# A graph transformer and a graph attention layer on one core: a new order for every step, and more buffers for five kinds of tiles

## Chip, cores and metric

The kernel runs on one core of a Trainium2 chip. The core has TensorE (PE), VectorE (DVE), ScalarE (ACT), GpSimd (POOL) and SyncE (SP), which here only issues DMAs. Each engine runs its own instructions strictly in the order in which the program lists them; engines wait for each other by semaphores. The metric is the device time of one execution in microseconds (us).

## What is computed

Two layers over 64 independent graphs of 256 nodes with 256 features. Layer 0 is a transformer layer whose attention is split by the value of the adjacency matrix; layer 1 is two graph attentions (GAT) and an FFN. Cut to what matters:

```python
# layer 0, per graph: x [256, 256], adj [256, 256]
q, k = heads(x @ Wq + bq), heads(x @ Wk + bk)                # 8 heads of 32
attn = softmax(q @ k.T / sqrt(32))
out  = sum(((attn * (adj == r)) @ heads(x @ Wv[r] + bv[r])) for r in range(4))
x1   = ln(x + merge(out) @ Wo + bo) * g1 + beta1
x2   = ln(x1 + gelu(x1 @ W1 + b1) @ W2 + b2) * g2 + beta2
# layer 1
def gat(h, W, a):
    Wh = h @ W
    e  = leaky_relu(Wh @ a[:256] + (Wh @ a[256:]).T, 0.2)
    return softmax(where(adj > 0, e, -9e15), axis=0) @ Wh
h  = ln(x2 + gat(gat(x2, gW1, ga1), gW2, ga2)) * g_ln1 + b_ln1
y  = ln(h + relu(h @ w_ff1 + b_ff1) @ w_ff2 + b_ff2) * g_ln2 + b_ln2
```

The adjacency holds only 0 and 1, so the kernel's main program handles those two values (a second program, for other values, stands behind a test and is not entered here).

## The kernel before

Weights stay in SBUF. There is no loop: the work of one graph is cut into some 210 named steps, and every step of every graph has a place, a number. `PLACES` gives the places for graph 0; graph g's step stands at `PLACES[name] + g * PERIOD`, with `PERIOD` 46.802. The program sorts all steps of all 64 graphs by place and emits them in that order. The places do nothing else: they are sort keys, and they set in which order each engine meets the steps of the six or seven graphs that are under way at once. The 49 weight loads (`LOAD_PLACES`) and the six pieces of weight preparation (`V_PLACE` and so on) are sorted into the same list. The numbers come from a search that was made beforehand.

The steps that the text names, in the order of the data, with the lines of the profile:

- `load`, `xT`, `cast`, `jT`, `no`: a graph's x and adjacency come in (L188, L190), are transposed (VectorE L527, a DMA transpose L543) and cast; `no` (GpSimd L550) is the mask of absent links for the GAT. `xS` (GpSimd L534): differences of blocks of x.
- `qk0`, `qk1`, `s0`, `s1` (TensorE L556, L604): queries and keys, and the scores of four heads each. `max`, `rec` (VectorE L609, L622), `exp`, `nrm` (ScalarE L617, L627): the softmax; the digits are the half m and the head h.
- `eT`, `eW`, `eR`: the attention is transposed in squares by VectorE (L338), written to DRAM and read back transposed (SyncE L343, L347). `pm` (VectorE L636) multiplies it by the adjacency: the mask. `po0`, `po1` (TensorE L651) and `oT0`, `oT1` (ScalarE L657): times the values.
- `vp1` to `vp7` (TensorE L580), `va` (VectorE L589), `vc1`, `vb`: the values, with seven products where eight blocks would be multiplied, and additions that put them together.
- `wo`, `ya` (TensorE L671, VectorE L675), `yb`: output projection and residual. Each layer norm n is `st` (VectorE L379), `rt`, `nb` (GpSimd L385 to L391), `ln` (ScalarE L396); `lg`, `lb` (GpSimd L363, L366) multiply and add its row vectors; `ag`, `ar`, `bg`, `br` are the same two operations on the residual of the FFN.
- FFN a (GELU): `aT`, `aW`, `aR` transpose as above; `at1` to `at4` (GpSimd L438) block differences; `ap1` to `ap7` (TensorE L453) seven products; `ac` (ScalarE L464) and `aa` (VectorE L470) put them together; `ax0` to `ax3` (ScalarE L476) the GELU; `aS1` to `aS4` (GpSimd L490) block differences of the hidden layer; `ad1` to `ad7` (TensorE L501) seven products; `ae`... (VectorE L509) add them to the residual. `tg` and `te` load ScalarE's tables.
- The GAT: `ga0`, `ga1`, `gac` (L681, L687), and for each of the two attentions A and B: `ip` (TensorE L693), `z` (ScalarE L700), `zl`, `zm`, `zx` (VectorE L703, L706, L710), `ze` (ScalarE L715), `zd` (L721, L723). `h1` and `h2` (TensorE L728, L743) are the products, `h1c`, `h2a` what reads them.
- FFN b (ReLU): `bu0` to `bu3` (TensorE L420), `bx0` to `bx3` (ScalarE L428), then `bS`, `bd`, `be` as in FFN a. `store` writes the result.

All products but the scores and a part of `ad` and `bd` share one kind of PSUM tile with three buffers (`ps_mm`); a step that opens one waits until the last reader of the buffer that it is given is done. The tiles that the change touches rotate in the same way in SBUF:

```python
plan += [(g * PERIOD + t, i, ops[n]) for i, (n, t) in enumerate(PLACES.items())]
with tc.manual_schedule():
    for _, _, f in sorted(plan, key=lambda p: p[:2]):
        f()
```

Of the kernel before, what the change touches and what calls it, by code (L numbers as in the profile page):

```python
# [9 lines left out]
F32 = mybir.dt.float32  # L10
# [8 lines left out]
P = 128  # L19
# [7 lines left out]

PERIOD = 46.802000
PLACES = {
    "load": 103.9751, "xT": 115.0053, "qk0": 126.6603, "qkc0": 127.1038, "s0": 134.9388, "max00": 136.7231,  # L30
    "qk1": 137.0310, "max03": 137.5321, "qkc1": 137.7942, "exp00": 138.1614, "max01": 140.5304, "rec00": 140.7033,
    "max02": 142.1718, "nrm00": 142.4292, "cast": 144.4484, "exp03": 147.8949, "eT00": 149.0132, "chk": 149.0607,
    "exp02": 149.5106, "exp01": 150.1354, "xS": 150.5393, "s1": 150.6950, "rec03": 150.7772, "nrm03": 151.8725,
    "max10": 153.8083, "max12": 153.8091, "max13": 154.4469, "eT03": 154.4477, "exp12": 154.6493, "eW03": 155.4630,
    "eW00": 156.5314, "rec01": 157.0565, "rec12": 158.9274, "rec02": 159.6382, "vp1": 161.4545, "nrm12": 165.5429,
    "max11": 166.0992, "vc1": 167.1785, "eT12": 168.1509, "nrm01": 168.3344, "jT": 169.8588, "eT01": 170.3657,
    "eW01": 171.0782, "exp10": 171.5535, "rec10": 172.2610, "exp13": 172.3736, "nrm10": 173.2351, "exp11": 174.3895,
    "eW12": 174.4820, "rec13": 177.1193, "eR03": 177.3099, "vp7": 177.3903, "vp6": 177.5917, "va6": 179.2791,
    "eR00": 179.4350, "va7": 180.4486, "nrm02": 180.6279, "eT10": 180.6555, "vb1": 180.6893, "nrm13": 180.6957,
    "vp5": 180.9267, "vp3": 181.2501, "va9": 181.6949, "eR01": 181.8420, "va5": 181.9831, "vp2": 182.0258,  # L40
    "va3": 182.1206, "va1": 182.7320, "eT02": 183.2926, "pm03": 183.3875, "vp4": 184.2094, "vb0": 187.0388,
    "va4": 187.0561, "eW02": 187.4248, "rec11": 187.7988, "eW10": 191.5046, "nrm11": 191.8443, "pm00": 193.2315,
    "eT13": 193.2323, "eR02": 195.3406, "eR10": 195.3413, "eT11": 196.6110, "pm01": 196.7514, "eW11": 197.3458,
    "y": 197.5444, "eW13": 204.3129, "pm02": 204.6352, "yb": 205.0770, "po0": 208.2558, "eR12": 211.7882,
    "pm10": 212.6028, "oT0": 213.3684, "pm12": 214.4221, "eR11": 215.4498, "eR13": 216.1883, "pm11": 220.8456,
    "pm13": 220.8464, "po1": 223.4844, "oT1": 225.7544, "wo": 226.4470, "ya": 228.2381, "st1": 228.8886,
    "rt1": 229.4475, "nb1": 229.9449, "ln1": 234.2672, "aT": 235.2647, "aW": 236.2517, "aR": 238.9482, "ag": 240.6661,
    "no": 243.1288, "at1": 243.2863, "at2": 243.3266, "ap1": 243.3672, "ap2": 243.9675, "ac1": 244.5699,
    "aa1": 245.3645, "ap6": 245.5386, "at3": 245.5532, "ac6": 247.4691, "at4": 247.9916, "ap7": 249.4691,
    "ar": 250.1780, "ap5": 250.3386, "ac7": 251.1468, "ap4": 251.5565, "aa7": 252.0569, "tg": 252.3489,  # L50
    "ap3": 252.4143, "ac4": 252.8450, "ax2": 253.7964, "aa6": 254.2113, "ax1": 256.9508, "ax0": 257.6471,
    "ax3": 257.7639, "aS1": 258.7003, "ad3": 259.1637, "ad5": 259.9822, "aS3": 260.0841, "aS2": 262.1691,
    "aS4": 262.4552, "ad1": 263.5703, "ad2": 263.5711, "ad7": 263.9317, "ad4": 265.6786, "ae": 265.7449,
    "ae1": 265.8658, "ae7": 266.1487, "ad6": 268.6987, "ae5": 269.4279, "ae6": 270.1012, "st2": 270.8366,
    "rt2": 272.8796, "nb2": 273.1259, "ln2": 275.0005, "lg2": 275.7094, "lb2": 276.1999, "hT": 276.2183,
    "hW": 280.2443, "hR": 282.2631, "ga0": 286.1421, "gac0": 286.2674, "ga1": 287.3134, "gac1": 287.4355,
    "ipA": 288.1844, "zA": 289.1647, "zlA": 290.9172, "zmA": 291.1840, "zxA": 291.3282, "zeA": 291.6948,
    "zdA": 291.8669, "h11": 293.6066, "h1c1": 294.2718, "h10": 295.3741, "h1c0": 297.1199, "ipB": 300.5575,
    "zB": 301.7395, "zlB": 303.5479, "zmB": 305.6801, "zxB": 305.9925, "zeB": 307.1002, "zdB": 307.5894,
    "h2": 312.8984, "h2a": 314.0704, "st3": 314.3871, "rt3": 315.0224, "nb3": 315.1133, "ln3": 316.3769,  # L60
    "bT": 317.8919, "bW": 321.5395, "bR": 322.2639, "bu1": 325.2576, "bu2": 326.9960, "bu0": 327.5659,
    "bx1": 327.8946, "bx2": 329.2876, "bu3": 329.6912, "bx0": 331.5281, "bg": 331.6469, "bx3": 332.3820,
    "br": 332.4081, "bS1": 332.4186, "bS2": 333.5718, "bd2": 334.8469, "bd3": 335.4834, "bd1": 335.5398,
    "bd6": 337.5839, "bS4": 340.4945, "bd5": 341.7280, "bS3": 342.6638, "be1": 344.6857, "be5": 345.2702,
    "be6": 345.5198, "bd4": 345.5393, "be": 346.8470, "bd7": 348.0359, "be7": 352.7953, "st4": 354.0792,
    "rt4": 357.7556, "nb4": 358.8382, "ln4": 359.6426, "lg4": 360.6282, "lb4": 364.9129, "store": 373.7957,
    "te": 514.9914,
}
LOAD_PLACES = [
    125.120, 106.258, 229.103, 150.870, 221.650, 221.641, 121.253, 228.780, 150.186, 119.871, 234.573, 232.294,  # L70
    235.866, 110.479, 215.936, 228.515, 130.114, 111.029, 155.377, 140.012, 185.331, 143.483, 182.314, 212.997,
    230.654, 163.446, 107.882, 259.336, 191.755, 270.022, 292.790, 266.477, 296.907, 276.387, 282.416, 241.872,
    305.973, 195.716, 294.339, 290.783, 243.026, 150.865, 294.400, 260.745, 293.271, 285.343, 296.910, 299.560,
    242.862,
]
V_PLACE, OUT_PLACE, FFA_PLACE, GAT_PLACE, FFB_PLACE, ODD_PLACE = 133.293, 191.755, 242.862, 282.414, 309.485, 240.000

# [11 lines left out]
def binary_graphs(  # L91
# [14 lines left out]
    B, N, D = x.shape  # L106
# [6 lines left out]
    C = N // P  # L113
# [6 lines left out]
    ap = ctx.enter_context(tc.tile_pool(name="attn", bufs=2))  # L120
    bp = ctx.enter_context(tc.tile_pool(name="dense", bufs=2))
# [29 lines left out]
    def weight(w, name, mixed=False):  # L151

        k, n = w.shape[0] // P, w.shape[1]
        t = const.tile([P, k, n], F32, name=name)
        if mixed:
            mixed_rows(t, w)
        else:
            loads.append((t, w.rearrange("(k p) n -> p k n", p=P)))
        return t
# [56 lines left out]
    wo, bo_r = weight(Wo, "wo"), rowvec(bo, D, "bo_r")  # L216
# [181 lines left out]
    class Ffn:  # L398
# [8 lines left out]
            self.t = self.xt = None  # L407

        def residual(self, src):
            self.r = bp.tile([P, C, D], F32, tag="res", name=f"{self.name}_res", bufs=3)  # L410
            times(self.r, src, self.gain)

        def residual_row(self):
# [17 lines left out]
        def node_sum(self, i):  # L431

            if self.xt is None:
                self.xt = bp.tile([P, 4, P], F32, tag="us", name=f"{self.name}_xt", bufs=1)
            (b11, b12), (b21, b22) = ([self.x.nodes(k)[:, j] for j in range(C)] for k in range(KD))
            t = [self.xt[:, j].rearrange("p (b y) -> p b y", y=S) for j in range(4)]
            o, a, b = {1: (t[0], b12, b11), 2: (t[1], b22, t[0]), 3: (t[2], b22, b12), 4: (t[3], b21, t[1])}[i]
            nc.gpsimd.tensor_tensor(o, a, b, ALU.subtract)  # L438
# [72 lines left out]
    class Graph:  # L511
# [99 lines left out]

        def exponential(self, m, h):
            n = f"{self.g}_{m}_{h}"
            self.e[m, h] = e = ap.tile([P, C, N], F32, tag="e", name=f"e{n}", bufs=4)
            self.den[m, h] = small.tile([P, C], F32, tag="den", name=f"den{n}")
            for ic in range(C):
                nc.scalar.activation(e[:, ic, :], self.s4[m][h][:, ic * N:(ic + 1) * N], AF.Exp,  # L617
                                     bias=self.nmax[m, h][:, ic:ic + 1], accum_out=self.den[m, h][:, ic:ic + 1])
# [8 lines left out]
                nc.scalar.activation(e[:, ic, :], e[:, ic, :], AF.Copy, scale=self.rden[m, h][:, ic:ic + 1])  # L627

        def squares(self, m, h):
            self.et[m, h] = Transposed(f"eT{self.g}_{m}_{h}", ap, "eT", 6)  # L630
            self.et[m, h].squares(self.e[m, h])

        def masked(self, m, h):
            t = self.et[m, h].t
            self.pm[m, h] = ap.tile([P, C, C, P], F32, tag="pm", name=f"pm{self.g}_{m}_{h}", bufs=4)
            nc.vector.tensor_tensor(self.pm[m, h].rearrange("p c k (b y) -> p (c k) b y", b=A),  # L636
                                    t.rearrange("p b c k y -> p (c k) b y"),
                                    self.adT.rearrange("p c k (b y) -> p (c k) b y", b=A), ALU.mult)
# [480 lines left out]
```

## Time and profile before

| | us |
|---|---|
| median of 3 runs | 3193.67 (3193.63 to 3193.97) |
| the profiled execution, and its span | 3193.6, 3191.7 |
| TensorE busy in the span | 3050.3 |
| span 0 to 167.4: TensorE busy | 129.0 of 167.4 |
| span 167.4 to 2981.5: TensorE busy | 2761.4 of 2814.1 |
| span 2981.5 to 3191.7: TensorE busy | 159.9 of 210.2 |

The three windows are the filling of the pipeline, the part in which every graph repeats the same pattern, and the draining. In the middle, windows of equal length one period apart show the same rows at the same distance, so one period stands for all. A row of a timeline gives the start, the length, the engine, the line, the tiles and the number of instructions that were merged; in brackets is the time that the engine idled before it and what ended the wait. The length of a matmul row is modelled, so the distance between starts is the better measure there.

### The profile page before, as it was taken

How to read it: one execution, taken by the hardware profiler on the slowest of the kernel's cores; microseconds unless marked ns; L12 is line 12 of the kernel's file. 1: busy time of each engine (PE TensorE's matmuls, PEld its weight loads, DVE VectorE, ACT ScalarE, POOL GpSimd, SP SyncE). 2: the span in 40 equal slices, each digit the busy share in tenths (PEclk: the TensorE clock that was granted, in tenths of full speed). 3: DMA queues.
4: the chain of work that ended last, by engine and by line, in shares of the span. 5: the costliest groups of instructions: out<-in, count | busy, mean ns of one | idle time of the engine just before them, and what ended most of it. 6: DMA issues, size and time to landing. Idle time of an engine off the chain costs nothing. (4 is left out here: it accounts for less than half of the span.)

```text
span 3191.7 us, 67685 instructions
## 1 busy us (share of the span) xinstructions
PE 3050.3 (96%) x23261; PEld 2626.8 (82%) x23261; DVE 2521.3 (79%) x5349; ACT 2479.2 (78%) x6853; POOL 2336.9 (73%) x2886
## 2 busy tenths in 40 slices
PE   6899999999999999999999999999999999999985
PEld 4788888888888888888888888888888888888774
DVE  6788888888878888888888888888888888888852
ACT  5678878878878877878887887887787787787752
POOL 2477777777777777777777777777777777777763
PEclk7999999999999999999999999999999999999997
DMA  6554455455455455455455455455455455455421
GB/s 190 156 151 141 145 154 145 140 154 147 142 151 147 141 152 150 139 153 152 136 155 151 138 152 152 138 149 153 137 150 154 138 147 154 142 143 154 136 63 31
DMA packets 808349, 456.88 MB, mean 143 GB/s; under 512 B 334528, under 2 KB 717376, under 8 KB 808000
## 3 DMA queue, kind: packets, MB, share of 16 engines
q1 hardware_dynamic: 808000, 452.49, 48.8%
q8 instruction: 187, 3.06, 0.4%
q14 instruction: 162, 1.33, 0.1%
HBM read 242.63 MB, written 201.33 MB: 139 GB/s over the span
## 5 line engine op out<-in xcount | busy, mean ns | idle before, releaser
L617 ACT ACTIVATE e<-s,nmax 128x256 f32<-128x256 f32 x1024 | 474.5, 480 | 73.0 <-DVE nmax L609 70.6
L420 PE MATMUL ffb_ps<-ffb_T,f 128*128 128x256 f32 x2048 | 459.2, 383 | 26.3 <-DMA ffb_T<-ffb_T_d 26.3
L627 ACT ACTIVATE e<-e,rden 128x256 f32<-128x256 f32 x1024 | 455.7, 503 | 11.6 <-DVE rden L622 11.6
L420 PEld LDWEIGHTS ffb_ps<-ffb_T,f 128*128 128x128 f32 x2048 | 389.9, 192 | 86.3 <-issue 17.2
L636 DVE TENSOR_TENSOR pm<-eT,adT 128x512 f32<-128x512 f32 x512 | 429.3, 849 | 4.3 <-DMA eT<-eT_d 3.7
L338 DVE STREAM_TRANSPOSE eT_sq<-e 128x512 f32<-128x512 f32 x512 | 359.7, 703 | 60.1 <-ACT e L627 35.8
L609 DVE TENSOR_REDUCE nmax<-s 128x2 f32<-128x512 f32 x512 | 331.4, 678 | 7.1 <-PE s L604 4.3
L565 ACT ACTIVATE qT<-qk_ps,bqs_c 128x256 f32<-128x256 f32 x128 | 60.7, 474 | 306.5 <-PE qk_ps L556 306.4
L490 POOL TENSOR_TENSOR ffa_t<-ffa_h 128x512 f32<-128x512 f32 x64 | 81.8, 1279 | 292.4 <-DVE gb_z L706 258.8
L428 ACT ACTIVATE ffb_h<-ffb_ps,bf_c 128x256 f32<-128x256 f32 x512 | 209.6, 483 | 28.4 <-PE ffb_ps L420 27.9
L476 ACT ACTIVATE ffa_h<-ffa_h,b_c 128x256 f32<-128x256 f32 x512 | 217.7, 501 | 2.2
L617 ACT ACTIVATION_READ_ACCUMULATOR e<-s,nmax 128x1 f32 x1024 | 216.7, 212 | 0.0
L386 POOL TENSOR_TENSOR rs_x<-rs_x,nhalf 128x2 f32<-128x2 f32 x256 | 200.7, 784 | 21.3
L490 POOL TENSOR_TENSOR ffa_t<-ffa_h,ffa_t 128x512 f32<-128x512 f32 x128 | 195.1, 1524 | 5.0
L490 POOL TENSOR_TENSOR ffb_t<-ffb_h 128x512 f32<-128x512 f32 x64 | 82.0, 1281 | 156.5 <-ACT ffb_h L428 156.5
L589 DVE TENSOR_TENSOR v<-v,v_ps 128x256 f32<-128x256 f32 x448 | 174.4, 401 | 10.1 <-PE v_ps L580 7.9
L396 ACT ACTIVATE ffa_res<-ffa_res,nb_x,rs_x 128x256 f32<-128x256 f32 x256 | 139.8, 593 | 54.5 <-POOL nb_x L391 54.5
L464 ACT COPY ffa_h<-ffa_ps 128x512 f32<-128x512 f32 x256 | 148.8, 581 | 41.3 <-PE ffa_ps L453 40.8
L490 POOL TENSOR_TENSOR ffb_t<-ffb_h,ffb_t 128x512 f32<-128x512 f32 x128 | 163.4, 1277 | 21.0 <-ACT ffb_h L428 20.8
L509 DVE TENSOR_TENSOR ffb_res<-ffb_po,ffb_res 128x256 f32<-128x256 f32 (+2 forms) x256 | 132.9, 519 | 53.0 <-issue 24.0
L470 DVE TENSOR_TENSOR ffa_h<-ffa_ps,ffa_h 128x512 f32<-128x512 f32 x192 | 131.5, 685 | 42.3 <-PE ffa_ps L453 42.2
L604 PE MATMUL s<-kT,qT 32*128 32x256 f32 x2048 | 151.9, 407 | 11.5 <-ACT e L617 10.6
(178 smaller groups left out, 8968.9 us busy)
## 6 DMA issues: line engine op xcount, KB each, us to landing
eT_d<-eT_sq SPq DMA_DIRECT2D x512, 256.0 KB, 2.4
eT<-eT_d SPq DMA_DIRECT2D x512, 256.0 KB, 3.3
xin<-in_x_dram SPq DMA_DIRECT2D x256, 64.0 KB, 4.0
adi<-in_adj_dram SPq DMA_DIRECT2D x64, 256.0 KB, 3.3
y<-in_x_dram SPq DMA_DIRECT2D x64, 256.0 KB, 4.9
ffa_T_d<-ffa_T_sq SPq DMA_DIRECT2D x64, 256.0 KB, 2.0
ffa_T<-ffa_T_d SPq DMA_DIRECT2D x64, 256.0 KB, 2.9
hT_d<-hT_sq SPq DMA_DIRECT2D x64, 256.0 KB, 2.0
```

The source lines that it names most:

```text
L338: nc.vector.transpose(self.sq.rearrange("p a c k y -> p (c k) a y"), src.rearrange("p c (k a x) -> p (c k) a x", k=KD, a=A))
L386: nc.gpsimd.tensor_tensor(self.rs, self.rs, nhalf, ALU.pow)
L420: nc.tensor.matmul(p[:, f - f0, :], self.wa[:, k, f * P:(f + 1) * P], self.x.nodes(k), start=(k == 0), stop=(k == KD - 1))
L428: nc.scalar.activation(self.h[half][:, f1 + f, :], self.ps[f0][:, f, :], self.func, bias=self.ba[:, f0 + f:f0 + f + 1])
L476: nc.scalar.activation(h, h, self.func, bias=self.ba[:, f0 + f:f0 + f + 1])
L490: nc.gpsimd.tensor_tensor(out, a, b, ALU.subtract)
L589: nc.vector.tensor_tensor(self.v_part(*to), self.v_part(*src), self.ps["v", i], ALU.add)
L604: nc.tensor.matmul(self.s4[m][h][:, ic * N:(ic + 1) * N], self.qT[hp, m, ic * P:(ic + 1) * P], self.kT[hp, m, :], start=True, stop=True)
L609: nc.vector.tensor_reduce(self.nmax[m, h], self.s4[m][h].rearrange("p (c n) -> p c n", c=C), AX.X, ALU.max, negate=True)
L617: nc.scalar.activation(e[:, ic, :], self.s4[m][h][:, ic * N:(ic + 1) * N], AF.Exp, bias=self.nmax[m, h][:, ic:ic + 1], accum_out=self.den[ ...
L627: nc.scalar.activation(e[:, ic, :], e[:, ic, :], AF.Copy, scale=self.rden[m, h][:, ic:ic + 1])
L636: nc.vector.tensor_tensor(self.pm[m, h].rearrange("p c k (b y) -> p (c k) b y", b=A), t.rearrange("p b c k y -> p (c k) b y"), self.adT.re ...
```

## The change

Every place is new: `PLACES`, `LOAD_PLACES` and the six single places come from another run of the search, in which the durations of GpSimd and VectorE operations were lengthened at random. `PERIOD` stays. No instruction is added or removed. Five kinds of tiles get more buffers: the residual of the FFNs 3 to 4, the block differences of FFN a 1 to 2, the exponentials 4 to 5, the transposed attention 6 to 8, the masked attention 4 to 6. The places fill most lines of the diff; here they are cut, and the orders that come of them follow.

```diff
 PERIOD = 46.802000
 PLACES = {
-    "load": 103.9751, "xT": 115.0053, "qk0": 126.6603, "qkc0": 127.1038, "s0": 134.9388, "max00": 136.7231,
...
+    "ap5": 252.0678, "ac7": 252.8866, "aa7": 253.1941, "ap4": 254.0429, "ac4": 254.1691, "ap3": 254.1718,
+    "ax3": 254.1722, "ag": 255.0296, "aa6": 255.1163, "ar": 255.8601, "ax1": 256.0262, "ax0": 257.6282,
...
-V_PLACE, OUT_PLACE, FFA_PLACE, GAT_PLACE, FFB_PLACE, ODD_PLACE = 133.293, 191.755, 242.862, 282.414, 309.485, 240.000
+V_PLACE, OUT_PLACE, FFA_PLACE, GAT_PLACE, FFB_PLACE, ODD_PLACE = 118.304, 188.933, 191.889, 235.795, 244.531, 240.000
...
-            self.r = bp.tile([P, C, D], F32, tag="res", name=f"{self.name}_res", bufs=3)
+            self.r = bp.tile([P, C, D], F32, tag="res", name=f"{self.name}_res", bufs=4)
...
-                self.xt = bp.tile([P, 4, P], F32, tag="us", name=f"{self.name}_xt", bufs=1)
+                self.xt = bp.tile([P, 4, P], F32, tag="us", name=f"{self.name}_xt", bufs=2)
...
-            self.e[m, h] = e = ap.tile([P, C, N], F32, tag="e", name=f"e{n}", bufs=4)
+            self.e[m, h] = e = ap.tile([P, C, N], F32, tag="e", name=f"e{n}", bufs=5)
...
-            self.et[m, h] = Transposed(f"eT{self.g}_{m}_{h}", ap, "eT", 6)
+            self.et[m, h] = Transposed(f"eT{self.g}_{m}_{h}", ap, "eT", 8)
...
-            self.pm[m, h] = ap.tile([P, C, C, P], F32, tag="pm", name=f"pm{self.g}_{m}_{h}", bufs=4)
+            self.pm[m, h] = ap.tile([P, C, C, P], F32, tag="pm", name=f"pm{self.g}_{m}_{h}", bufs=6)
```

The order of one period on TensorE, from qk0 on (steps of several graphs, as they follow each other):

```
before  qk0 ad6 po1 vp7 vp6 wo vp5 vp3 s0 vp2 qk1 vp4 bu1 bu2 bu0 bu3 ga0 ga1 bd2 ipA bd3 bd1 ap1 ap2 bd6 s1
        ap6 h11 bd5 h10 ap7 ap5 ap4 bd4 ap3 ipB bd7 po0 vp1 ad3 ad5 ad1 ad2 ad7 ad4 h2
after   qk0 ad6 vp6 vp2 po1 vp7 vp5 vp4 s0 wo vp3 qk1 bu1 bu2 bu0 bu3 ga1 ga0 bd2 ipA bd1 s1 bd3 ap1 ap2 bd6
        ap6 h11 bd5 h10 ap7 ap5 ap4 ap3 ipB bd4 bd7 po0 vp1 ad3 ad2 ad1 ad7 ad5 ad4 h2
```

Parts of the order on the other engines, around the steps that feed these:

```
ScalarE  before  qkc1 exp00 te ln1 bx1 bx2 nrm00 bx0 nrm11 bx3 gac0 gac1 exp03 zA exp02 exp01 ac1 zeA zdA nrm03
                 ac6 h1c1 exp12 h1c0 ac7 tg ac4 ax2 zB ax1 ax0 ax3 nrm12 oT0 zeB vc1 zdB
         after   exp00 nrm11 nrm10 qkc1 exp03 exp01 te bx2 ln1 bx1 bx0 exp02 bx3 gac1 gac0 zA nrm03 zeA ac1 zdA
                 tg h1c1 ac6 ln4 h1c0 ac7 nrm00 ac4 ax3 zB ax1 ax0 ax2 zeB nrm01 vc1 zdB oT0
VectorE  before  aa7 rec12 rec02 be aa6 xT zlB zmB zxB be7 pm10 max11 st4 pm12 eT12 eT01 ae
         after   aa7 eT00 be6 xT aa6 pm12 zlB zmB be zxB max11 be7 pm13 st4 pm11 pm10 eT01 ae
GpSimd   before  bg cast br bS1 bS2 ag no at1 at2 xS at3 bS4 at4 bS3 ar yb aS1 aS3 aS2 aS4 rt4 nb4 lg4 rt3 nb3
         after   bg rt1 nb1 cast no vb0 br bS1 bS2 at1 bS4 at2 at3 bS3 at4 yb ag ar lg4 aS1 aS3 aS2 aS4 rt4 nb4
                 xS lb4 rt3 nb3
```

On SyncE's queue the reads eR11, eR12 and eR13 move ahead, eR10 moves back, and the store moves from behind bR to before bW. In the filling, OUT (the output bias) stays next to the second graph's qk0, and the weight preparation of FFN a (FFA) moves from the third graph's to the second's, that of the GAT and of FFN b by 46.6 and 65.0 in place.

## Prediction

> **What bounds the kernel now.** I read the page first, then TensorE's waits, then the timeline of one period on TensorE and on the three engines that feed it.
>
> ```profile
> span 3191.7 us, 67685 instructions
> PE 3050.3 (96%) x23261; PEld 2626.8 (82%) x23261; DVE 2521.3 (79%) x5349; ACT 2479.2 (78%) x6853; POOL 2336.9 (73%) x2886
> ...
> PE ffa_pq L501 <- POOL ffa_t L490: 53.0, 62, 0.9
> PE ffb_ps L420 <- DMA ffb_T<-ffb_T_d: 26.3, 6, 10.4
> ```
>
> TensorE is busy 96% and is short of work for only 141.4 us (3191.7 − 3050.3). 53.0 of these are one wait that comes once per graph: ad4 (`ffa_pq`) for the last of four GpSimd subtractions (aS4, `ffa_t`). The second line is the drain: six waits, not a rhythm.
>
> ```profile
> 1524.13 1.16 PE L453 MATMUL ffa_ps<-ffa_xt,w 128*128 128x128 f32 x8
> 1525.13 1.06 PE L501 MATMUL ffb_pq<-f,ffb_t 128*128 128x128 f32 x8
> 1526.02 1.06 PE L453 MATMUL ffa_ps<-ffa_T,ffa_u 128*128 128x128 f32 x8
> 1526.91 0.38 PE L693 MATMUL gb_ips<-ident,gb_wh 128*128 128x128 f32 x2
> ...
> 1534.09 1.06 PE L501 MATMUL ffa_po<-w,ffa_h 128*128 128x128 f32 x8
> 1536.01 1.16 PE L501 MATMUL ffa_pq<-w,ffa_t 128*128 128x128 f32 x8 [0.86 <-POOL ffa_t L490]
> ...
> 1583.66 1.16 PE L501 MATMUL ffa_pq<-w,ffa_t 128*128 128x128 f32 x8 [0.86 <-POOL ffa_t L490]
> ```
>
> Columns: start, length, engine, line, tiles. The rows are ap4, bd4, ap3, ipB, ad7, ad4, and ad4 one graph later. One graph takes 1583.66 − 1536.01 = 47.65 us. A group of eight of these matmuls advances TensorE by 0.89 (1525.13 to 1526.02); ad7 to ad4 is 1.92, so 1.03 is lost per period. TensorE has no other gap in that period, so whatever is moved on other engines counts only through such gaps.
>
> ```profile
> 1527.34 0.84 ACT L700 ACTIVATE gb_z<-gb_ips,gb_wh 128x256 f32<-128x256 f32 x2 [0.32 <-PE gb_ips L693]
> 1528.07 2.49 ACT L476 ACTIVATE ffa_h<-ffa_h,b_c 128x256 f32<-128x256 f32 x6
> ...
> 1529.89 1.28 POOL L490 TENSOR_TENSOR ffa_t<-ffa_h 128x512 f32<-128x512 f32 x1 [4.33 <-DVE gb_z L706]
> 1531.25 1.60 POOL L490 TENSOR_TENSOR ffa_h<-ffa_h,ffa_h 128x512 f32<-128x512 f32 x1
> 1532.82 3.14 POOL L490 TENSOR_TENSOR ffa_t<-ffa_h,ffa_t 128x512 f32<-128x512 f32 x2
> ...
> 1530.81 0.91 DVE L636 TENSOR_TENSOR pm<-eT,adT 128x512 f32<-128x512 f32 x1
> 1534.13 0.69 DVE L636 TENSOR_TENSOR pm<-eT,adT 128x512 f32<-128x512 f32 x1
> ```
>
> This is the chain that ends in ad4. ScalarE waits for ipB, runs zB, then the GELUs ax1, ax0 (two instructions each, 2.49/6 = 0.415), and aS1 starts 0.16 after ax0 (1528.07 + 4 × 0.415 = 1529.73, against 1529.89; the VectorE name in that row had little to do with it). aS1, aS3, aS2 and aS4 then run without a break until 1535.96: 6.07 us. Two masks (pm, VectorE) fall among them. Where no mask does, such a subtraction lasts 1.28 (first row); aS3 under the first mask lasts 1.60, and aS2 and aS4 with the second 3.14 instead of the 2.62 of the pair without one, in the fill:
>
> ```profile
> 145.28 2.62 POOL L490 TENSOR_TENSOR ffa_t<-ffa_h,ffa_t 128x512 f32<-128x512 f32 x2
> ```
>
> **The sum.** I count from the end of ap4, 1525.13, called 0.
>
> TensorE. Between ap4 and ad4 both kernels run the same groups (bd4, ap3, ipB, bd7, po0, vp1 and five of ad); the order alone differs: before bd4, ap3, ipB; after ap3, ipB, bd4. Work: 1534.98 (end of ad7, 1534.09 + 0.89) − 1525.13 = 9.85. So ad4 is due at 9.85; before it came at 10.88.
>
> Chain, after. ipB moves up by one group, but ScalarE can't use all of it, since ax3 now stands before zB. ac4 starts 0.26 after ap4 ends (before, after ap7: 1523.50 against 1523.24) and takes 0.57; ax3 0.83; zB 0.73 (1527.34 to 1528.07): done at 2.39. ax1 also needs aa6 on VectorE, which now follows aa7, eT00, be6 and xT: aa7's 0.61 ends its turn at −0.11, then 0.62 + 0.48 + 0.64 puts aa6 at 1.63 and its 0.69 ends at 2.32, just in time. ax1 and ax0 take 1.66: 4.05; aS1 starts at 4.2 (before: 4.76). With the old 6.07, aS4 ends at 10.27 and ad4 starts 0.05 later (as 1535.96 to 1536.01), at 10.32: lost 0.47, where 1.03 was lost. Bounds: with no mask among the four, 6.07 − 0.32 − 0.52 = 5.23 gives 9.48 and nothing is lost; with a third mask at 0.52 it is 10.84, and 0.99 is lost. I take 6.07, the row of the same four instructions: three masks (pm13, pm11, pm10) now follow zlB on VectorE, but the last two stand behind st4 and may come after aS4 has begun. Saved: 0.56.
>
> New waits. ap3 stands directly behind ap4, and needs aa7 to have read the bank that ap5 filled: aa7 ended at 1525.09, 0.04 before ap4's end, so 0.05 lost. vp5 is now allotted the bank that oT1 empties: po1's end + 0.25 + 0.36 + 0.05 against 0.53 of vp7, 0.13 lost; but wo, which in the old order waits for the same copy (vp6 to wo takes 0.56 instead of 0.43), now comes five groups later: nothing net. bd2 needs bx3: after bu2 ScalarE runs bx2, ln1, bx1, bx0, exp02, bx3: 0.26 + 0.72 + 0.98 + 1.42 + 0.91 + 0.86 + 0.05 = 5.20, while TensorE runs bu0, bu3, ga1, ga0: 2 × 1.73 + 1.75 = 5.21. No cover is left; I charge 0.06 and keep 0 to 0.8.
>
> Work that goes elsewhere at no cost: ag and the mask of absent links (1.72 + 1.93 on GpSimd) leave the stretch before at1; they go behind at4 and before bS1, where GpSimd waited 4.33 and 2.23. ln4 (1.09 on ScalarE) moves a graph later, between ac6 and h1c0, where ScalarE waits 0.29 to 0.57 at a time; its cover is the 0.87 of h10, and beyond that ap5 waits for h1c0. More buffers add no instruction and no wait: the counts of every engine are equal in both programs. On SyncE's queue the reads eR11 to eR13 move up behind the next graph's load (five issues, 4.01 + 1.18) and eR10 moves down behind them; pm10, last of the masks, waits for it, and behind pm10 only eT01 and ae. The store now stands before bW and waits for lb4; lb4 precedes rt3 on GpSimd, and bT, which bW needs, comes only after rt3, nb3 and ln3.
>
> Fill and drain. The windows of 167.4 and 210.2 us at the ends hold 38.4 and 50.3 of TensorE's idle time. The weight work of both FFNs and of the graph attention moves a stage or more forward (a row of 4.46 on TensorE, nine operations of 7.4 on VectorE): a gain of 8 if it hides, a loss of 8 if it delays the first softmaxes; I take 0. From qk0 to be7 the plan grows by 228.35 − 226.14 = 2.2: +2 in the drain.
>
> Sum: 59 periods (2814.1 / 47.65) × (−0.56 + 0.05 + 0.06 = −0.45) = −26.6; + 2: −24.6. The profiled run took 3193.6 around its span of 3191.7, and the median is 3193.67, so no correction: 3169.
>
> The row speaks for 0.32 and 0.52 per mask. The Trainium skill, SBUF — State Buffer, "Who interferes with whom", speaks against this change: a VectorE instruction with two SBUF inputs and a GpSimd instruction that reads SBUF exclude each other for the whole instruction. If all three masks blocked for their full 0.65, ad4 would lose 5.23 + 1.95 + 4.25 − 9.85 = 1.58, and the kernel would be slower by 59 × (1.58 − 1.03 + 0.11) + 2 = 41 us; the two masks in the trace cost 0.84 together and not 1.30, which is why the rows are used.
>
> **Rivals.** (a) The masks miss the chain: nothing lost at ad4, −1.03 + 0.11 = −0.92 per period, −54 + 2: 3141. For it: masks behind st4 may come late. Against: in this period both were caught.
> (b) The wait only changes shape: third mask, 0.99 lost, −0.04 + 0.11 = +0.07 per period, + 4 + 2: 3199.7, within 0.2% (6.4 us, what can be told from no change here).
> (c) Slower: bd2 becomes the wait. ScalarE must start bx2 within 0.01 us of its earliest time. Before it stand exp03 and exp01, whose maxima follow hT, st1 and va3 on VectorE, and hT follows lb2 on GpSimd. I work out 0.8 of reserve there; two masks caught (0.84) or a late lb2 eat it. From 0.06 + 0.45 = 0.51 of lateness the kernel is slower; at 0.85 it is 59 × 0.34 + 2 = + 22: 3215. For it: the wait grows one for one. Against: ScalarE's row of idle time is 22% of the span.
>
> **How the numbers follow.** Forecast 0.42, (a) 0.15, (b) 0.15, (c) with its like (vp4 behind va1, ap6 behind ac1) 0.28. The likeliest case's own range is 3157 to 3183. The range over the cases is 3140 to 3215. Faster 0.57, same 0.15, slower 0.28.
>
> **What would show it.** Right: `ffa_pq <- POOL ffa_t` falls from 53.0 to some 20 to 30 in all, the period is 47.2, the fill ends within 8 us of 167. Wrong: that wait stays near 50 (b), or a new line of 30 or more stands on `ffb_pq <- ACT ffb_h` (c), on `v_ps`, or on `ffa_ps <- DVE ffa_h`; or the two ends of the span move by more than 10.

## The result, and the profile after

The changed kernel takes 3157.51 us (median of four runs, 3154.80 to 3157.55), the kernel before 3193.82 beside it: ratio 0.9882, with a 95% interval of 0.9864 to 0.9899. That is 36.3 us less. The forecast was 24.6 less, 3169, with 3140 to 3215 as its range; the measured time lies at the lower edge of the likeliest case's own range, 3157 to 3183. The profiled execution took 3157.49 around a span of 3155.7.

The page of the changed kernel (its line numbers are one lower than before: L490 is now L489, L501 is L500):

```profile
span 3155.7 us, 67642 instructions
...
PE 3058.0 (97%) x23261; PEld 2621.5 (83%) x23261; DVE 2484.2 (79%) x5349; ACT 2473.6 (78%) x6853; POOL 2266.0 (72%) x2886
```

TensorE's waits in the changed kernel, then one line of its weight loads (PEld) in the kernel before and the same line in the changed kernel, in total us, times, longest:

```profile
PE ffb_ps L419 <- DMA ffb_T<-ffb_T_d: 20.5, 3, 10.3
...
PE ffa_pq L500 <- POOL ffa_t L489: 1.6, 3, 0.6
```

```profile
PEld ffa_pq L501 <- POOL ffa_t L490: 65.1, 63, 1.1
```

```profile
PEld ffa_pq L500 <- POOL ffa_t L489: 19.1, 63, 0.8
```

Of 53.0 us the wait of ad4 for aS4 seems to leave 1.6. It does not: it is now so short that it stands almost wholly on the weight load, 19.1 in 63 times where 65.1 stood before. The starts on TensorE's timeline tell what is still lost. One period of the changed kernel, at ap4, ap3, ipB, bd4, then ad5, ad4, and ad5, ad4 one graph later:

```profile
1509.22 1.13 PE L452 MATMUL ffa_ps<-ffa_xt,w 128*128 128x128 f32 x8
1510.18 1.12 PE L452 MATMUL ffa_ps<-ffa_T,ffa_u 128*128 128x128 f32 x8
1511.14 0.38 PE L692 MATMUL gb_ips<-ident,gb_wh 128*128 128x128 f32 x2
1511.36 1.06 PE L500 MATMUL ffb_pq<-f,ffb_t 128*128 128x128 f32 x8
...
1519.21 1.06 PE L500 MATMUL ffa_po<-w_t,ffa_t 128*128 128x128 f32 x8
1520.36 1.16 PE L500 MATMUL ffa_pq<-w,ffa_t 128*128 128x128 f32 x8
...
1566.18 1.06 PE L500 MATMUL ffa_po<-w_t,ffa_t 128*128 128x128 f32 x8
1567.33 1.16 PE L500 MATMUL ffa_pq<-w,ffa_t 128*128 128x128 f32 x8
```

A graph takes 1567.33 − 1520.36 = 46.97 us, where it took 47.65. ad5 to ad4 is 1.15 where a group advances TensorE by 0.89: 0.26 is lost there, and 1.03 was. The chain that ends in ad4, on ScalarE, GpSimd and VectorE of the changed kernel:

```profile
1511.82 0.82 ACT L699 ACTIVATE gb_z<-gb_ips,gb_wh 128x256 f32<-128x256 f32 x2
1512.53 2.49 ACT L475 ACTIVATE ffa_h<-ffa_h,b_c 128x256 f32<-128x256 f32 x6
```

```profile
1514.30 1.28 POOL L489 TENSOR_TENSOR ffa_t<-ffa_h 128x512 f32<-128x512 f32 x1 [4.86 <-PE po L650]
1515.67 1.27 POOL L489 TENSOR_TENSOR ffa_h<-ffa_h,ffa_h 128x512 f32<-128x512 f32 x1
1516.89 3.41 POOL L489 TENSOR_TENSOR ffa_t<-ffa_h,ffa_t 128x512 f32<-128x512 f32 x2
```

```profile
1512.26 0.67 DVE L635 TENSOR_TENSOR pm<-eT,adT 128x512 f32<-128x512 f32 x1
...
1516.24 1.24 DVE L635 TENSOR_TENSOR pm<-eT,adT 128x512 f32<-128x512 f32 x1
...
1518.33 2.52 DVE L635 TENSOR_TENSOR pm<-eT,adT 128x512 f32<-128x512 f32 x2
```

Counted from the end of ap4 (1510.18), zB now starts at once at 1.64 (before at 2.21, with 0.32 of waiting for ipB), aS1 at 4.12 (before 4.76), and the four subtractions take 6.00 (before 6.07). Three masks lie beside them: pm13 on aS3 and aS2, pm11 and pm10 on aS2 and aS4. aS3 is not lengthened, the pair aS2 and aS4 takes 3.41 where 2.62 is its time alone, and the masks themselves are stretched: 1.24 and 2.52 for one and for two, where a free one takes 0.67.

From the fifth graph's qk0 to the last's (59 periods) the time falls from 2814.0 to 2773.2, by 40.8. The filling before it grows from 155.2 to 160.8, the rest behind it goes from 222.5 to 221.7. −40.8 + 5.6 − 0.8 = −36.0, the change of the span.

### The profile page after: what moved, and what is told of

Same layout as the page of the kernel before. It is cut to its first block, busy times and chain, and to the rows that moved or that the text cites. A ratio compares the mean times of both kernels' runs of the same rounds, so it can differ in the third digit from the quotient of the medians.

```text
span 3155.7 us, 67642 instructions
## 1 busy us (share of the span) xinstructions
PE 3058.0 (97%) x23261; PEld 2621.5 (83%) x23261; DVE 2484.2 (79%) x5349; ACT 2473.6 (78%) x6853; POOL 2266.0 (72%) x2886
## 4 chain that ended last, share of the span: by engine, by line
PE 81%; POOL 12%; DMA 2%; DVE 2%; ACT 1%; issue 1%; SPq 1%; POOLq 0%; DVEq 0%; ACTq 0%
PE ffb_ps L419 14%; PE ffa_ps L452 13%; POOL ffa_t L489 9%; PE ffb_po L500 7%; PE qk_ps L555 7%; PE v_ps L579 6%; PE ffb_pq L500 6%; PE po L650 6%; PE s L603 4%; PE wo_ps L670 4%; PE h_ps L727 4%; PE ga_wps L680 4%; PE h_ps L742 3%; POOL ffa_h L489 3%; PE ffa_pq L500 2%; PE ffa_po L500 2%
## 5 line engine op out<-in xcount | busy, mean ns | idle before, releaser
L635 DVE TENSOR_TENSOR pm<-eT,adT 128x512 f32<-128x512 f32 x512 | 467.0, 923 | 0.8 <-DMA eT<-eT_d 0.8
L608 DVE TENSOR_REDUCE nmax<-s 128x2 f32<-128x512 f32 x512 | 339.7, 676 | 1.1 <-PE s L603 1.1
L489 POOL TENSOR_TENSOR ffa_t<-ffa_h 128x512 f32<-128x512 f32 x64 | 82.5, 1289 | 309.3 <-PE po L650 278.8
L489 POOL TENSOR_TENSOR ffa_t<-ffa_h,ffa_t 128x512 f32<-128x512 f32 x128 | 210.8, 1647 | 5.0
L702 DVE SCALAR_TENSOR_TENSOR ga_z<-ga_z 128x512 f32<-128x512 f32 x64 | 46.2, 721 | 194.3 <-ACT ga_z L699 194.3
L385 POOL TENSOR_TENSOR rs_x<-rs_x,nhalf 128x2 f32<-128x2 f32 x256 | 181.9, 710 | 21.3
L384 POOL TENSOR_SCALAR rs_x<-mv_x 128x2 f32<-128x2 f32 x256 | 76.5, 299 | 152.1 <-DVE mv_x L380 136.3
L489 POOL TENSOR_TENSOR ffb_t<-ffb_h,ffb_t 128x512 f32<-128x512 f32 x128 | 163.8, 1280 | 9.5 <-ACT ffb_h L427 1.1
L489 POOL TENSOR_TENSOR ffb_t<-ffb_h 128x512 f32<-128x512 f32 x64 | 99.7, 1557 | 93.2 <-ACT ffb_h L427 93.2
```

Of the source, the lines that this page charges most:

```text
L489: nc.gpsimd.tensor_tensor(out, a, b, ALU.subtract)
L608: nc.vector.tensor_reduce(self.nmax[m, h], self.s4[m][h].rearrange("p (c n) -> p c n", c=C), AX.X, ALU.max, negate=True)
```

## The experiments

Each kernel was timed against the kernel before on the same chip, which took 3196.3 to 3197.3 in these series, so the ratios are to be compared. Spans and periods are of the profiled executions; a period is the median distance of successive qk0 in the part where every graph repeats (before 47.65, changed 46.98).

**1. The buffers alone.** The kernel before with the five larger numbers of buffers.

```diff
-            self.r = bp.tile([P, C, D], F32, tag="res", name=f"{self.name}_res", bufs=3)
+            self.r = bp.tile([P, C, D], F32, tag="res", name=f"{self.name}_res", bufs=4)
...
-            self.pm[m, h] = ap.tile([P, C, C, P], F32, tag="pm", name=f"pm{self.g}_{m}_{h}", bufs=4)
+            self.pm[m, h] = ap.tile([P, C, C, P], F32, tag="pm", name=f"pm{self.g}_{m}_{h}", bufs=6)
```

> The kernel before with its own places and the five larger numbers of buffers. Theory (the new order alone makes the gain, since TensorE's only periodic wait in the kernel before is for a GpSimd subtraction and not for a free buffer): 3193.7, within 3 us. Rival (the buffers make the gain, the order only happens to be new): 3157, and the wait of ffa_pq for ffa_t gone. A mixture would lie between.

Measured: 0.9996 (0.9987 to 1.0005), period 47.63, the wait of ad4 51.7 in all. The buffers by themselves, in the old order, do nothing; the gain is the order's.

**2. One step moved in the kernel before,** bd4 on TensorE, with be, which reads its result on VectorE, behind it.

```diff
-    "bd4": 345.5393, "be": 346.8470,
+    "bd4": 347.4595, "be": 352.5821,
```

> The kernel before with one step of FFN b moved: bd4 stands behind ipB instead of ahead of ap3 (and be, which adds its result, behind zmB). Theory (ipB comes one group earlier, so zB no longer waits for it, and bd4 fills TensorE's time while the chain runs): the chain zB, ax1, ax0, aS gets 0.42 us earlier, ap3 waits 0.05 for aa7, so 59 x 0.37 = 22 less: 3172, within 5; the wait of ffa_pq for ffa_t falls from 53 to about 30 in all. Rival (ScalarE's and VectorE's new orders carry the gain, TensorE's order alone gives nothing): 3194. Rival on the other side (be, moved behind zmB, holds a bank too long): above 3198, with a new wait on TensorE.

Measured: 0.9917 (0.9904 to 0.9931), span 3169.7, period 47.22. The wait fell to 16.9 in the row, and by the starts ad4 now loses 0.45:

```profile
1525.17 1.06 PE L501 MATMUL ffa_po<-w,ffa_h 128*128 128x128 f32 x8
1526.51 1.16 PE L501 MATMUL ffa_pq<-w,ffa_t 128*128 128x128 f32 x8 [0.28 <-POOL ffa_t L490]
```

That is 0.58 less than before, of which ap4 and ap3, which now follow each other directly, give back 0.12 (1.02 and 0.99, where they took 1.00 and 0.89). So bd4's place (with be's, two of the 224 entries of `PLACES`) makes 22 of the 36 us. be's own place was not tried apart; in the kernel before and in this run ax1 follows zB at once, so nothing in the chain waits for it. Here are ap3, which starts where ap4 ends, ac4 and aS1:

```profile
1516.08 1.16 PE L453 MATMUL ffa_ps<-ffa_T,ffa_u 128*128 128x128 f32 x8
```

```profile
1516.43 0.57 ACT L464 COPY ffa_h<-ffa_ps 128x512 f32<-128x512 f32 x1
```

```profile
1520.39 1.28 POOL L490 TENSOR_TENSOR ffa_t<-ffa_h 128x512 f32<-128x512 f32 x1 [3.94 <-PE po L651]
```

aS1 starts at 4.31 after ap4's end: 0.19 later than in the changed kernel, and the subtractions take the old 6.07. 0.19 is also what ad4 loses more than there (0.45 against 0.26).

**3. The table load ahead as well.** In the kernel before, tg stands between ac7 and ac4, and ac4 starts 0.35 after ap4's end in run 2. In the changed kernel tg comes earlier and ac4 starts at 0.20.

```diff
-    "tg": 252.3489,
+    "tg": 251.1368,
```

(with the two lines of run 2)

> As the run with bd4 moved, and the table load tg of ScalarE stands ahead of ac7 instead of between ac7 and ac4. Theory (tg made ac4 start 0.17 later after ap4's end than in the changed kernel): another 59 x 0.17 = 10 less than the run with bd4 alone: 3162. Rival (tg now makes ac7 late, which ap3 needs for its bank): slower than the run with bd4 alone, with a wait of ffa_ps for ffa_h. No change between the two would say that tg was hidden.

Measured: 1.0065 (1.0051 to 1.0079). The rival holds: ac7 now comes behind the table load, and ap4 waits for the bank that it empties, once per graph (42.9 us in 63 times). My expectation named ap3 for this wait; it is one group earlier:

```profile
1533.55 1.06 PE L453 MATMUL ffa_ps<-ffa_xt,ffa_u 128*128 128x128 f32 x8
1535.27 1.16 PE L453 MATMUL ffa_ps<-ffa_xt,w 128*128 128x128 f32 x8 [0.67 <-ACT ffa_h L464]
```

tg needs a place farther ahead, as the changed kernel gives it (behind zdA). What stands behind ap4 shows tg's part all the same (ap3, ac4, aS1):

```profile
1536.27 1.06 PE L453 MATMUL ffa_ps<-ffa_T,ffa_u 128*128 128x128 f32 x8
```

```profile
1536.47 0.59 ACT L464 COPY ffa_h<-ffa_ps 128x512 f32<-128x512 f32 x1 [1.25 <-PE ffa_ps L453]
```

```profile
1540.44 1.27 POOL L490 TENSOR_TENSOR ffa_t<-ffa_h 128x512 f32<-128x512 f32 x1 [4.62 <-PE po L651]
```

ac4 starts at 0.20 after ap4's end, as in the changed kernel, and aS1 at 4.17: 0.14 of the 0.19 is tg's. The other 0.05 stays open; it lies between the GELUs and aS1. ad4 still loses 0.44 in this run, since ap3 and ipB now take 0.89 and 0.22 instead of 0.99 and 0.25, and TensorE is ready as much earlier.

**4. The step put back in the changed kernel.**

```diff
-    "bd4": 350.4209, "be": 352.3587,
+    "bd4": 347.7069, "be": 348.7153,
```

> The changed kernel with bd4 put back ahead of ap3 and be back ahead of aa6, all else as changed. Theory: zB waits for ipB again and the chain ends 0.3 to 0.45 later, ap3's 0.05 is saved: 59 x 0.25 to 0.4 = 15 to 24 more, 3172 to 3181, and the wait of ffa_pq for ffa_t is back at 30 to 40 in all. Rival (the gain sits in the other engines' orders): 3157, within 3.

Measured: 0.9998 (0.9989 to 1.0007), span 3193.9, period 47.55. The whole gain is gone, more than expected. ScalarE and TensorE of this kernel:

```profile
1531.11 0.84 ACT L699 ACTIVATE gb_z<-gb_ips,gb_wh 128x256 f32<-128x256 f32 x2 [0.48 <-PE gb_ips L692]
```

```profile
1537.87 1.06 PE L500 MATMUL ffa_po<-w_t,ffa_t 128*128 128x128 f32 x8
1539.66 1.16 PE L500 MATMUL ffa_pq<-w,ffa_t 128*128 128x128 f32 x8 [0.73 <-POOL ffa_t L489]
```

zB waits for ipB again, aS1 comes at 4.71, and ad4 loses 1539.66 − 1537.87 − 0.89 = 0.90. I had expected the chain to end 0.3 to 0.45 later; it begins 0.59 later and ends 0.57 later. All the other moves of the change together leave 0.10 per period (47.65 to 47.55), and the filling takes that back.

**5. Two masks moved off the subtractions.** pm13 and pm11 ahead of zlB.

```diff
-    "pm13": 214.3210, "pm11": 217.4995,
+    "pm13": 211.0152, "pm11": 211.0352,
```

> The changed kernel with the masks pm13 and pm11 moved ahead of zlB on VectorE, where GpSimd waits, so that of the three masks beside aS1 to aS4 only pm10 is left. Theory (a mask beside a GpSimd subtraction lengthens it; ad4 still loses 0.26 per period): the four subtractions take 5.5 to 5.75 instead of 6.00, ad4 is due on time, 59 x 0.25 = 15 less: 3143, VectorE's masks shorter in the mean (0.92 now). Rival on the other side (zlB, zmB, zxB come 1.2 later, so zeB, zdB and h2 do): above 3165, with a wait of h_ps for gb_wh on TensorE of 0.2 or more per period. Rival (what the masks gain is lost elsewhere): 3157.

Measured: 1.0877 (1.0862 to 1.0892), 319 us more than the changed kernel by the span. None of the three expected cases holds: VectorE waits for po0 in front of a mask (101.5 us in 62 times), and be behind it holds the bank that ad3 opens (204.2 us in 60 times, 3.4 each). The mean granted clock fell to 0.946, from 0.984 in the changed kernel; run 6 and the last section follow such a stop. A graph's first four masks are read by po0, the others by po1. With six buffers the fifth and the sixth find a free one; the seventh, pm11, must wait until po0 has read the first.

**6. The old numbers for three kinds.** The changed kernel with 1, 6 and 4 buffers for the block differences, the transposed attention and the masked attention; the residual's 4 and the exponentials' 5 stay (their old numbers were not tried with this order).

```diff
-            self.et[m, h] = Transposed(f"eT{self.g}_{m}_{h}", ap, "eT", 8)
+            self.et[m, h] = Transposed(f"eT{self.g}_{m}_{h}", ap, "eT", 6)
...
-            self.pm[m, h] = ap.tile([P, C, C, P], F32, tag="pm", name=f"pm{self.g}_{m}_{h}", bufs=6)
+            self.pm[m, h] = ap.tile([P, C, C, P], F32, tag="pm", name=f"pm{self.g}_{m}_{h}", bufs=4)
```

> The changed kernel with the old number of buffers for the block differences of FFN a (1), the transposed attention (6) and the masked attention (4); the residual keeps 4 and the exponentials 5. Theory (places make the gain, the buffers only allow the order): 3157, within 4. Rival (some of these three are needed for the order to run without waits: at2 behind ap5's read of the old tile, pm waiting for po): 3165 or more, and the wait is seen on GpSimd (ffa_xt <- PE) or VectorE (pm <- PE).

Measured: 1.0944 (1.0929 to 1.0959), span 3499.1. The rival holds: with four buffers pm12, the fifth mask, waits for po0, and be behind it comes late for ad3. VectorE, ad3 on TensorE, then TensorE's windows (us, busy, granted clock, then the share and GB/s of the DMA engines):

```profile
1517.62 0.65 DVE L469 TENSOR_TENSOR ffa_h<-ffa_ps,ffa_h 128x512 f32<-128x512 f32 x1
1521.12 0.94 DVE L635 TENSOR_TENSOR pm<-eT,adT 128x512 f32<-128x512 f32 x1 [2.85 <-PE po L650]
```

```profile
1525.14 1.77 PE L500 MATMUL ffa_pq<-w_t,ffa_h 128*128 128x128 f32 x8 [3.41 <-DVE ffb_res L508]
```

```profile
1521.50:1525.10 3.60, 0.23 (x2) 1.00 0.98 301
1525.14:1528.41 3.27, 3.27 (x16) 0.55 0.13 28
1530.40:1532.20 1.80, 1.80 (x18) 1.00 0.57 178
```

TensorE stands for 3.57 us more than its work ahead of ad3, and then two groups and a double group take 1.57, 1.70 and 2.00 instead of 0.89, 0.89 and 1.78, at a granted clock of 0.55: 1.71 more. 3.57 + 1.71, less the 0.36 that ad4 no longer costs (run 10 shows these 0.36), is 4.92; the median period grew by 52.20 − 46.98 = 5.22, and the 0.30 between them was not followed. Three kinds were put back here; run 7 says which of them counts.

**7. Two kinds back.** As run 6, with the masked attention at 6.

```diff
-            self.pm[m, h] = ap.tile([P, C, C, P], F32, tag="pm", name=f"pm{self.g}_{m}_{h}", bufs=4)
+            self.pm[m, h] = ap.tile([P, C, C, P], F32, tag="pm", name=f"pm{self.g}_{m}_{h}", bufs=6)
```

> The changed kernel with the old number of buffers for the block differences of FFN a (1) and the transposed attention (6) alone; the masked attention keeps 6. Theory (in the run with three kinds put back, pm12 on VectorE waited 2.85 for po0 to give a mask's buffer back, and that wait alone made the 342): 3157, within 4. Rival (the reads of the attention on SyncE's queue, which waited 1116 in all for po there, are late by themselves): several tens or hundreds more, with a wait of po for eT on TensorE or of pm for eT on VectorE.

Measured: 0.9965 (0.9952 to 0.9979), span 3183.1: 27 more than the changed kernel, where run 6 had 343, and not the 3157 that I expected. The masked attention's buffers make all but these 27: they let this order run without run 6's stop, though in the old order they did nothing. SyncE's queue waits for po here, where the changed kernel has 0.4 in all:

```profile
SPq L346 <- PE po L650: 954.0, 188, 12.7
```

The reads of the attention come only when po has given a tile back. The shortest periods are those of the changed kernel (46.95 to 46.98), but among them stand 51.78, 51.05, 49.30, 48.87 and many of 47.1 to 47.7, where the changed kernel has one above 47.4 (47.85). That the late reads let single slow transfers through to TensorE is the likely reading; no single delay was followed to its transfer.

**8. The weight preparation back.** FFN a's and the GAT's at the distance of the kernel before.

```diff
-V_PLACE, OUT_PLACE, FFA_PLACE, GAT_PLACE, FFB_PLACE, ODD_PLACE = 118.304, 188.933, 191.889, 235.795, 244.531, 240.000
+V_PLACE, OUT_PLACE, FFA_PLACE, GAT_PLACE, FFB_PLACE, ODD_PLACE = 118.304, 188.933, 241.142, 280.694, 244.531, 240.000
```

> The changed kernel with the weight preparation of FFN a and of the GAT back at the distance from the first graph's qk0 that it has in the kernel before. Theory (the 5.6 that the filling lost come from this work standing ahead of the first softmaxes on VectorE and ScalarE): the fifth qk0 comes at 155 instead of 160.8, 3152, within 2. Rival (they come from the order of the loads and reads on SyncE's queue): 160.8 and 3157, within 2. Rival on the other side (one stage later it stands in the way of more): 3160 or more.

Measured: 0.9873 (0.9858 to 0.9888), the fifth qk0 at 160.14. The third and fourth qk0 come 1.7 and 5.2 earlier (57.35 and 107.47), the stage behind them gives 4.5 back. So this work is not what the filling lost; runs with the changed places but for one or two had the fifth qk0 at 160.0 to 162.7. Loads and reads on SyncE's queue remain as a suspect, and so does the preparation of FFN b and of the values, which kept its new place here; that stays open.

**9. The GELUs in another order.** ax3 behind ax0, xT behind aa6.

```diff
-    "ax3": 254.1722, "xT": 114.7095,
+    "ax3": 257.9000, "xT": 114.7303,
```

> The changed kernel with ax3 behind ax0 on ScalarE (aS1 needs only ax0 and ax1) and xT behind aa6 on VectorE. Theory: zB starts when ipB is done, about 0.4 earlier, ax1 and ax0 follow, aS1 starts at 3.75 after ap4's end instead of 4.12; aS3, which needs all four GELUs (done at 5.27), starts at 5.32 instead of 5.49; ad4 loses 0.09 instead of 0.26: 59 x 0.17 = 10 less, 3147. Rival (aS3 waits longer, or a later mask falls on the longer pair): 3157. Rival on the other side: xT behind aa6 delays xS or qk0, above 3160, with a wait of qk_ps for xT.

Measured: 0.9914 (0.9900 to 0.9928), slower than the changed kernel; period 47.09. zB starts only 0.21 earlier, at 1.43, since it now waits 0.65 for ipB; all four GELUs end at 5.45, not at the 5.27 that I expected, and aS3 waits for them and starts at 5.60 instead of 5.49: 0.11 later, as the period. I had expected zB 0.4 earlier, and that is what failed.

**10. One mask moved.**

```diff
-    "pm13": 214.3210,
+    "pm13": 211.0152,
```

> The changed kernel with the mask pm13 alone moved ahead of zlB (pm12 and pm13 are the fifth and the sixth mask of their graph, so six buffers let them through before po0). Theory (in the run with pm13 and pm11 moved, pm11 as the seventh waited for po0; the move of a mask as such is harmless): no wait of pm for po, and pm13 no longer beside aS2: between 3142 and 3157, since pm11 and pm10 come 1.2 earlier and still fall beside aS2 and aS4. Rival (moving any mask ahead of zlB delays be, the z steps and ad3): 3200 or more.

Measured: 0.9812 (0.9798 to 0.9825), 3137.17: faster than both kernels, and below my bounds. GpSimd, VectorE and TensorE of this kernel:

```profile
1503.91 1.28 POOL L489 TENSOR_TENSOR ffa_t<-ffa_h 128x512 f32<-128x512 f32 x1 [4.74 <-PE po L650]
1505.28 1.27 POOL L489 TENSOR_TENSOR ffa_h<-ffa_h,ffa_h 128x512 f32<-128x512 f32 x1
1506.50 2.62 POOL L489 TENSOR_TENSOR ffa_t<-ffa_h,ffa_t 128x512 f32<-128x512 f32 x2
```

```profile
1501.87 1.27 DVE L635 TENSOR_TENSOR pm<-eT,adT 128x512 f32<-128x512 f32 x2
...
1508.19 2.08 DVE L635 TENSOR_TENSOR pm<-eT,adT 128x512 f32<-128x512 f32 x2
```

```profile
1508.81 1.06 PE L500 MATMUL ffa_po<-w_t,ffa_t 128*128 128x128 f32 x8
1509.70 1.06 PE L500 MATMUL ffa_pq<-w,ffa_t 128*128 128x128 f32 x8
1510.60 0.60 PE L742 MATMUL h_ps<-gb_wh,gb_z 128*128 128x256 f32 x2
```

pm12 and pm13 run as a pair while GpSimd waits. pm11 still falls beside aS4, yet all four subtractions are clean: 5.21 from 1503.91 to 1509.12. The mask pays (1.48, last section); pm10 starts behind it, when aS4 is done, and the two take 2.08. ad4 follows ad5 by 0.89: nothing is lost. And ad4's own group now takes 0.90 (1509.70 to 1510.60) instead of the 0.99 that it takes behind a wait. 0.26 + 0.10 = 0.36 per period, 59 × 0.36 = 21; the span fell by 21.4. I had counted the gap, not the group behind it.

**11. All three masks moved off.** As run 10, and pm11 and pm10 behind ae7.

```diff
-    "pm11": 217.4995, "pm10": 217.8848,
+    "pm11": 220.2086, "pm10": 220.2186,
```

> As the run with pm13 alone, and pm11 and pm10 moved behind ae7, so that no mask is left beside aS1 to aS4. Theory (the masks cost GpSimd's four subtractions 0.75 of their 6.00, and ad4 still loses 0.26): aS takes 5.25, ad4 comes on time, 59 x 0.26 = 15 less: 3142, within 4. Rival on the other side (pm11 and pm10 push st3, ae5, ae6 and va6 back by 1.3, and po1 needs both): above 3160, with a wait of po for pm or of v_ps for v on TensorE. Rival (off the masks, another mover lengthens the subtractions): 3157 with aS at 6.00.

Measured: 1.0153 (1.0139 to 1.0167). The subtractions are as clean as in run 10, so nothing was left to gain, and the second rival holds: TensorE waits for the copies of the values that VectorE now makes later, and for oT1, 62.8 us in all:

```profile
1520.56 0.67 PE L579 MATMUL v_ps<-wv,xs 128*128 128x256 f32 x2 [0.36 <-DVE v L588]
1521.71 0.70 PE L579 MATMUL v_ps<-wv_t,xs 128*128 128x256 f32 x2 [0.48 <-ACT oT L656]
```

**12. Both moves at once.** The lines of run 4 and of run 10 together.

```diff
-    "bd4": 350.4209, "be": 352.3587, "pm13": 214.3210,
+    "bd4": 347.7069, "be": 348.7153, "pm13": 211.0152,
```

> The changed kernel with both moves: bd4 back ahead of ap3 (that alone cost 38) and pm13 ahead of zlB (that alone gained 20). Theory (two independent ways to give ad4 back what it waits: TensorE's order sets when the chain begins, the masks set how long the four subtractions take): the chain begins at 4.71 after ap4's end as in the run with bd4 back, the four subtractions take 5.21 as in the run with pm13 moved, ad4 starts at 9.97 where TensorE is ready at 9.85: 0.12 lost and 0.10 in the group behind the gap, 0.12 of ap3's wait saved, a period of 46.72, 59 x 0.87 = 51 less than the run with bd4 back: 3144, within 4. Rival (without bd4 behind ipB the masks' place is worth no more than the 20 that it gained in the changed kernel): 3176. Rival (pm11 and pm10 fall on aS2 and aS4 in another way when the chain comes later, and lengthen them again): 3160 to 3190, with the pair at 3.1 to 3.4.

Measured: 0.9873 (0.9857 to 0.9890), span 3155.5, period 46.89. The mask alone gives 38 with bd4 in its old place (3193.9 to 3155.5), against 21 with bd4 moved: both feed the same wait, and what one has taken the other can't take again. The chain comes as reckoned: aS1 at 4.70, the four clean in 5.20. The period is 0.17 above the 46.72 that I expected. Against run 10 it is 0.27 longer: 0.10 in vp5 and vp4 and 0.23 in the groups of ad, most of it in ad1 and ad4 (0.99 each instead of 0.89), less 0.06 at ap3. For ad4 the reason is known: it begins 0.05 after the end of aS4, which it needs. ad4 follows ad5 without a gap, but I had not counted that a group that just catches its operand is slower, nor the 0.10. The time lies outside what I expected (3140 to 3148) and outside both rivals.

## Why the prediction was right, and where it was not

**The bound and the gap: right.** Everything that the change does in the repeating part it does through TensorE's gaps, and almost all through ad4's. The 59 periods became 40.8 shorter, the whole span 36.0.

**The term of ad4: right mechanism, too small.** Forecast −0.56 per period, measured 1.03 − 0.26 = −0.77. The beginning of the chain was reckoned well: zB ends at 2.35 (forecast 2.39), aS1 starts at 4.12 (4.20). The four took 6.00 (6.07), so ad4 started at 10.18, not 10.32: 0.14. The rest is the due time. I set it at 9.85 and charged ap3's wait apart, but ap3 stands ahead of the gap: its 0.06 only moves the due time to 9.92 and comes out of what ad4 waits. A delay in front of a gap on the same engine is paid only if the chain is delayed too. By the runs, bd4's place makes 0.58 of the 0.77 (run 2; 0.64 in run 4). Of the 0.19 by which aS1 then still came late, tg makes 0.14 (run 3); it stood in my chain as "0.26 after ap4 ends" without being named.

**The masks: the value held by luck, the reasoning did not.** I took 6.07 on the ground that two of three masks might come late. All three came in time, and the sum stayed because VectorE paid most of it: the mean of a mask rose from 0.85 to 0.92, and aS3's from 1.59 fell to 1.29. I treated 0.32 and 0.52 as prices of a mask, and put the rule of mutual exclusion aside because two masks had cost 0.84 and not 1.30. The last section shows that the rule gives these rows to within 0.14. A fixed price per mask doesn't exist; what counts is which of the two instructions is running when the other comes. Rival (a), nothing lost at ad4, was within one place of being true: run 10 is that case in its effect, 3137 where I gave it 3141, though one mask still meets aS4 there.

**New waits: right in size.** bd2's step grew by 0.07 (0.89 to 0.96; forecast 0.06) and ap3's by 0.06 (0.05). The six steps of the values ahead of bu1, which I put at nothing net, take 3.02 together, before 3.03. Rival (c), bd2 as the new bound, needed 0.51 there and got 0.07: ScalarE kept its reserve.

**Fill and drain: small, but not as reckoned.** The filling, forecast as 0 with ±8, came out at +5.6, and FFN a's and the GAT's preparation, which I had named for it, does not explain that (run 8); the draining, forecast as +2, at −0.8.

**"More buffers add no instruction and no wait": right and incomplete.** They add none (run 1), but I did not ask what the new order does without them. Five masks ahead of po0's end need more than four buffers; run 6 costs 343 us. For the sum it made no difference. For understanding the change it is half of it: the order is the gain, and the buffers are its condition.

**The sum.** −0.77 + 0.07 + 0.06, less 0.04 in small parts, is −0.68 a period; 59 of them are −40. Forecast −26.6 + 2. Every term of the period had its sign; the one that was mis-sized is ad4's, by 0.21, or 12 us. The ends of the span took some of it back: +4.8 where +2 was forecast.

## What to carry to other kernels

Where one engine is busy 96%, read the chain that ends in its only periodic gap, and count a move by what it does to that chain's start, to its length, or to the work that covers it: one step of TensorE (bd4), or one mask of VectorE (pm13), was worth some 38 us each in the changed kernel, but only some 60 together, and the same step 22 in the kernel before. Two engines that exclude each other should be read instruction by instruction, not by a mean. A change of order and a change of buffers belong together: try the order with the old buffers, and the old order with the new.

## What the runs showed of the hardware

**A mask and a GpSimd subtraction take turns, and the one that comes second pays.** In the kernel before, aS4 starts 0.03 after pm12 (1534.13, 0.69 long, shown in the prediction); pm12 keeps its time and aS4 takes 1.79:

```profile
1534.16 1.79 POOL L490 TENSOR_TENSOR ffa_t<-ffa_h,ffa_t 128x512 f32<-128x512 f32 x1
```

In the run with pm13 moved, aS4 is first (1507.85, 1.27 long, ending at 1509.12); pm11 comes 0.34 later and takes 1.48, that is, 0.93 until aS4 ends and 0.55 for itself (0.67 when it is free):

```profile
1508.19 1.48 DVE L635 TENSOR_TENSOR pm<-eT,adT 128x512 f32<-128x512 f32 x1
```

In the changed kernel they alternate: aS4 starts behind pm11 and waits for its end, and pm10, which comes 0.39 after aS4, waits for aS4's end at 1520.30:

```profile
1518.70 1.60 POOL L489 TENSOR_TENSOR ffa_t<-ffa_h,ffa_t 128x512 f32<-128x512 f32 x1
```

```profile
1519.09 1.75 DVE L635 TENSOR_TENSOR pm<-eT,adT 128x512 f32<-128x512 f32 x1
```

This is what the Trainium skill, SBUF — State Buffer, "Who interferes with whom", says: the lock is exclusive, and the order of issue decides who blocks. Each of these rows agrees with it: the rest of the first instruction plus the second's own free time gives 0.11 to 0.14 more than each row shows. What failed was my use of it: all waiting charged to GpSimd gave +41 us, while the same order, with VectorE as the second, cost far less.

**A short stop of TensorE costs its clock too.** Behind the stop of 3.57 us in run 6 the granted clock was 0.55 over the next 3.27 us, and 1.00 in the row from 1530.40; in the mean of the whole run it was 0.945, where the changed kernel has 0.984. The Trainium skill, TensorE: Matmul & The Clock Gate, Part 1 ("The HAM clock gate"), has a window of about 3.4 us of idleness after which the clock is halved. The stop agrees with it: it lies at that length, 3.41 as ad3's row gives the idle time and 3.57 by the starts. The kernel before, with 1.03 lost in every period, has 1.00 from 167.4 to 2981.5: gaps of that length leave the clock alone here.

**The group behind a wait is slower by 0.10.** Eight matmuls that wait for their operand advance TensorE by 0.99 (ad4 in most runs, ap4 before, ap3 in run 2), the same eight without a wait, behind another group of eight, by 0.89 or 0.90. It happens even where no idle time is shown in front of them: in run 12 ad4 follows ad5 without a gap and still takes 0.99. The 0.10 lies between the first two matmuls: in the changed kernel ad4's first weight load starts with its matmul (1520.35 and 1520.36), and the second matmul follows the first by 0.21; in run 10, where nothing is waited for, the load starts 0.11 ahead (1509.60 and 1509.70) and the second matmul follows by 0.11.
